# A message-passing kernel on one core: the turned table built first, and the shares of its column copies, row copies and gathers set anew

## The chip, the core and the metric

The kernel runs on one core of a Trainium2 chip. The metric is the device time of one execution in microseconds (us). A core has five engines with queues of their own: PE (matmul and transpose), DVE (VectorE), ACT (ScalarE), POOL (GpSimd) and SP, which here does nothing but issue DMAs. Each engine's sequencer takes its instructions in program order, loads registers and hands work to the engine.

## What is computed

```python
h = jnp.maximum(_layernorm(x, axis=-1), 0.0)          # 12500 nodes, 48 wide
x_i = h[dst]                                          # 400000 edges, dst sorted
x_j = h[src]
tmp = jnp.concatenate([x_i, x_j, edge_attr], axis=1)  # 48 + 48 + 32
msg = jax.nn.relu(tmp @ W1 + b1) @ W2 + b2            # hidden 128
out = x + jax.ops.segment_sum(msg, dst, num_segments=12500)
```

## The kernel before

**Tables first.** W1 splits in three. Ahead of the edges, `node_tables` normalizes the nodes in six slices (`centre`: mean and square; `scale`: variance, root, product), transposes them (`turn`, L170, into `ht`, with the ReLU) and multiplies: `table(j, wb, ...)` makes `tab_b`, the part by source, one row of 128 numbers for each node, `table(j, wa, ...)` makes `tab_a`, the part by destination with b1. Both go to DRAM through SP (L205). Beside that POOL gathers the raw x rows of the first chunks' edges (`xg`, L760), and turns `rel` into places inside a chunk's window. `squares`, `most` and `check` (L799 to L847) find out whether any edge lies outside its window and make addresses out of the index numbers.

**Edges in chunks.** Edges go in 391 chunks of 8 tiles of 128 (`T`, `CE`). Because dst is sorted, a chunk's destinations lie in a window of 80 nodes. For chunk c the loop of `windows` (L502) does, engine by engine in the order written there:

- SP (`prepare`, `rows`): loads of edge attributes (`lhs`), of destinations (`row`), of the window of `tab_a` (`rhs`), and one tile's share of row copies (`gs`, L289).
- POOL (L371): one indirect DMA for each tile that nobody else makes; it fetches 128 rows of `tab_b` into `gb`. `gp` has seven buffers.
- DVE: `lhs` (L379) one-hot of the window for the product with `rhs`, `hot` (L389) the same the other way round, `seg` (L460) the sum into the segment.
- PE: `before(c-1)` (L400) edge attributes and destination part into `pre`, `fold(c-2)` (L445, L448) the sum over edges into `p_g`, `gathered(c-1)` (L421) the source part added to `pre`.
- ACT: `hidden(c-1)` (L437), the ReLU.

**Four ways to the source part.** The source rows of a tile come in one of four ways. The first four chunks (`RAW`) take raw x, transposed and multiplied in the loop. All other tiles take a gather of POOL, row copies of SP (`gs`, 15 a chunk), or are built column by column out of `bt`, a copy of the table in SBUF with one column for each node: DVE and ACT each copy one column of 128 numbers for one edge (`columns`, L325 to L348). A chunk has 143 such copies in eleven parts (`PARTS`, L60): five on DVE (8, 15, 16, 20, 12) and six on ACT (12, 8, 8, 20, 12, 12). Ahead of each part the engine's own sequencer loads the part's addresses, one number for a copy, in multiples of four (L272); the place of the segment's sum is loaded with the part of 15. `bt` itself is made by `turn(i)` (L296), three blocks in each of the first chunks, out of `wb` and `ht`; copies start at chunk 5 (`COLS`).

**Segments.** Sums collect in two SBUF buffers (`segs`) by turns, twelve chunks each (`GQ`). At the change of segment DVE clears the new buffer (L476) and takes over the overlap (L478). During the next segment's first chunks PE multiplies the old one by W2 and b2 (L488, L489), DVE adds it to x (L495), SP stores it (L499).

The order of work on each engine is the order of the program (`manual_schedule`).

Of the kernel before, what the change touches and what calls it, by code (L numbers as in the profile page):

```python
# [40 lines left out]
RAW = 4  # L41
NRAW = RAW * T
RAW_PART = 16
# [8 lines left out]
TURNS = 3  # L52
BLOCKS = (NPAD + CE - 1) // CE
BUILD = (BLOCKS + TURNS - 1) // TURNS
COLS = BUILD
# [10 lines left out]
STRIP = 144  # L66
# [3 lines left out]
RPART = 15  # L70
BASE = 0

BT0 = 16512
SEG0 = 161696
# [3 lines left out]
AT_PLACE, AT_SEG, SEG, NEXT = 16, 17, 18, 19  # L78
WIDTH = 20
# [13 lines left out]
EPS = 1e-5  # L93

# [7 lines left out]
def node_tables(nc, tc, keep, x, ident, w1, b1, wb, ht, xg, ones, tab_a, tab_b, index, loads,  # L102
                squares, most, check):

    slices = [(0, 8), (8, 16), (24, 20), (44, 20), (64, 20), (84, 14)]
# [6 lines left out]
    with ExitStack() as es:  # L112
        node = es.enter_context(tc.tile_pool(name="node", bufs=3))
        sqp = es.enter_context(tc.tile_pool(name="sqp", bufs=2))
        ps_t = es.enter_context(tc.tile_pool(name="ps_t", bufs=3, space=PSUM))
        ps_n = es.enter_context(tc.tile_pool(name="ps_n", bufs=3, space=PSUM))
# [5 lines left out]
        wa = keep.tile([2 * D + 1, 2, HID], F32, name="wa")  # L122
        nc.vector.memset(wb, 0.0)
# [21 lines left out]
        sqs = {}  # L145

        def centre(j):
            r0, rb = slices[j]
            h = xs[j]
            of = total[:, r0 : r0 + rb]  # L150
            nc.vector.tensor_reduce(of, h, AX.X, ALU.add)
            nc.vector.scalar_tensor_tensor(
                h, of.unsqueeze(2).to_broadcast([P, rb, D]), -1.0 / D, h,
                op0=ALU.mult, op1=ALU.add,
            )
            sqs[j] = sqp.tile([P, rb, D], F32, name="sq")
            nc.scalar.activation(sqs[j], h, AF.Square)

        def scale(j):
            r0, rb = slices[j]  # L160
            h = xs[j]
            of = rstd[:, r0 : r0 + rb]
            var = node.tile([P, rb], F32, name="var")
            nc.vector.tensor_reduce(var, sqs.pop(j), AX.X, ALU.add)
            std = node.tile([P, rb], F32, name="std")
            nc.scalar.activation(std, var, AF.Sqrt, bias=eps, scale=1.0 / D)
            nc.vector.reciprocal(of, std)
            nc.vector.tensor_mul(h, h, of.unsqueeze(2).to_broadcast([P, rb, D]))

        def turn(j):  # L170
            r0, rb = slices[j]
            h = xs[j]
            for g in range(0, rb // 2, 4):
                n = min(4, rb // 2 - g)
                p_t = ps_t.tile([2 * D, 4, P], F32, name="p_t")
                for q in range(n):
                    nc.tensor.transpose(
                        p_t[:, q, :],
                        h[:, 2 * (g + q) : 2 * (g + q) + 2, :].rearrange("p r d -> p (r d)"),
                        ident,  # L180
                    )
                nc.scalar.activation(
                    ht[: 2 * D, r0 // 2 + g : r0 // 2 + g + n, :], p_t[:, :n, :], AF.Relu
                )

        def table(j, wt, tv, dve):

            r0, rb = slices[j]
            rows = wt.shape[0]
            t = node.tile([P, rb, HID], F32, name="tab")  # L190
            for g in range(0, rb // 2, 2):
                n = min(2, rb // 2 - g)
                p_n = ps_n.tile([P, 2, 2 * HID], F32, name="p_n")
                for q in range(n):
                    nc.tensor.matmul(  # L195
                        p_n[:, q, :], ht[:rows, r0 // 2 + g + q, :],
                        wt.rearrange("k a h -> k (a h)"), start=True, stop=True,
                    )
                to = t[:, 2 * g : 2 * (g + n), :].rearrange("p r h -> p (r h)")
                of = p_n[:, :n, :].rearrange("p q h -> p (q h)")  # L200
                if dve and g % 4:
                    nc.vector.tensor_copy(to, of)
                else:
                    nc.scalar.copy(to, of)
            nc.sync.dma_start(tv[:, r0 : r0 + rb, :], t)  # L205

        for i in range(ns + 3):
            if i < ns:
                centre(i)
            if 0 <= i - 1 < ns:  # L210
                scale(i - 1)
            if 0 <= i - 2 < ns:
                turn(i - 2)
            if i == ns:
                squares()
            if i == ns + 1:
                most()
            if i == ns + 2:
                check()
            if 0 <= i - 3 < ns:  # L220
                table(i - 3, wb, tb_v, i >= ns)
        late = {1: (centre, ns), 2: (scale, ns), 3: (centre, ns + 1), 4: (scale, ns + 1)}
        for j in range(ns):
            if j in late:
                of, k = late[j]
                of(k)
            table(j, wa, ta_v, True)


def windows(nc, tc, gp, bt, ident, idx, raw, rhss, x_t, tab_a, tab_b, dst, edge_t, w2s, b2s,  # L230
            sources, out_t):
# [3 lines left out]
    xg, wb, ht = raw  # L235
    with ExitStack() as es:
# [24 lines left out]
        gss = {}  # L261

# [30 lines left out]

        bt_v = bt.rearrange("h (p r) -> h r p", r=NR)

        def turn(i):  # L296

            n = min(T, NR - i * T)
            p_t = ps_p.tile([P, T, HID], F32, name="pre")
            parts = p_t.rearrange("h (k q) p -> h k q p", k=2)  # L300
            for k in range(2):
                nc.tensor.matmul(
                    parts[:, k, : n // 2, :].rearrange("h q p -> h (q p)"), wb[:, k, :],
                    ht[: 2 * D, i * T // 2 : (i * T + n) // 2, :].rearrange("k g p -> k (g p)"),
                    start=True, stop=True,
                )
            nc.scalar.copy(
                bt_v[:, i * T : i * T + n, :].rearrange("h (q k) p -> h q k p", k=2),
                parts[:, :, : n // 2, :].rearrange("h k q p -> h q k p"),
            )  # L310
# [14 lines left out]
        def columns(c, part):  # L325
# [15 lines left out]
            for k, of in enumerate(got[:n]):  # L341
                j, e = divmod(first + k, P)
                if j not in gts:
                    gts[j] = gtc.tile([HID, P], F32, name="gt")
                of = of.with_bounds(
                    min_val=BT0, max_val=BT0 + 4 * (N - 1), guaranteed_mod_val=0, out_of_modulus=4
                ) - BT0
                copy(gts[j][:, e : e + 1], bt8[:, bass.ds(of, 4)].bitcast(F32))  # L348

        def prepare(c):  # L350
# [10 lines left out]
            base, *nodes = numbers(c, BASE, 1 + m, mybir.EngineType.SP)  # L361
# [109 lines left out]
        def segment_next(g):  # L471

            old, new = segs[g % 2], segs[(g + 1) % 2]
            if g > 0:
                for k in range(2):
                    nc.vector.memset(new[:, k, W:], 0.0)  # L476
            of, = numbers(begin(g), NEXT, 1, mybir.EngineType.DVE)
            nc.vector.tensor_copy(  # L478
                new[:, :, :W], old[:, :, bass.ds(of.with_bounds(min_val=0, max_val=FAR), W)]
            )  # L480
# [20 lines left out]
        with tc.manual_schedule():  # L501
            for c in range(NCH + 2):  # L502
# [9 lines left out]
                columns(c, 1)  # L512
# [35 lines left out]
                for i in range(c * TURNS, min((c + 1) * TURNS, BLOCKS)):  # L548
                    turn(i)
# [130 lines left out]
def tile_gnn_preln(  # L680
# [15 lines left out]
    ones: bass.AP,  # L696
    w1: bass.AP,
# [38 lines left out]
    ht = const.tile([2 * D + 1, NR // 2, P], F32, name="ht")  # L736
# [11 lines left out]
    gp = ctx.enter_context(tc.tile_pool(name="gp", bufs=7))  # L748

    with tc.tile_pool(name="keep", bufs=1) as keep, tc.tile_pool(  # L750
# [14 lines left out]
        def loads():  # L765
# [12 lines left out]
            gather(0, RAW_PART)  # L778
# [7 lines left out]
            if NT > full * T:  # L786
# [3 lines left out]
                )  # L790

            nc.gpsimd.tensor_tensor(off[:, :2, :], far[:, 1:3, :], far[:, :2, :], op=ALU.subtract)
            nc.gpsimd.tensor_tensor(off[:, 2, :], off[:, 0, :], off[:, 1, :], op=ALU.add)
            nc.gpsimd.tensor_tensor(off[:, 3, :], off[:, 0, :], far[:, 3, :], op=ALU.add)
            nc.gpsimd.tensor_scalar_add(off, off, -MID)
            nc.gpsimd.tensor_tensor(far, off, off, op=ALU.mult)
            gather(RAW_PART, NRAW - RAW_PART)

        def squares():  # L799
# [135 lines left out]
```

## Time and profile before

| | us |
|---|---|
| median of 3 runs | 3365.4 (3362.72 to 3370.66) |
| the profiled execution | 3372.65 |
| its span, first to last instruction | 3370.8 |
| mean granted TensorE clock | 0.911 |

In the profile a group reads: line, engine, operation, tile written<-tiles read, shapes, xcount | busy us, mean ns of one | idle us of the engine just before them, and who ended it. A timeline row reads: start, duration, engine, line, operation, tiles, count and the idle time before it. A register load's row gives minimum, median and maximum in ns, then first and last start in us. "issue" is time in which nothing that the profile shows was waited for. Small instructions overlap at their ends: DVE's column copies show 144 ns each, but follow one another much faster.

### The profile page before, as it was taken

What the parts mean: (1) busy time and instruction counts of PE and PEld (TensorE: products, weight loads), DVE (VectorE), ACT (ScalarE), POOL (GpSimd) and SP (SyncE); (2) the same over time, 40 slices, a digit from 0 to 9 for tenths busy, and PEclk for the clock granted to TensorE, in tenths of its full rate; (3) what the DMA queues carried; (4) which work ended last, traced back from release to release, by engine and by line L of the source; (5) the groups of instructions that cost most, each with busy time, mean ns of one, the idle gap of its engine ahead of it and who ended that gap; (6) DMA issues with size and microseconds to landing.
All of it is one profiled execution on the core that took longest, in us unless ns stands there. A gap on an engine that the chain in (4) does not pass through costs nothing.

```text
span 3370.8 us, 115212 instructions
## 1 busy us (share of the span) xinstructions
PE 2775.6 (82%) x16394; PEld 2158.3 (64%) x16394; DVE 2800.1 (83%) x29140; ACT 3035.6 (90%) x28179; POOL 2530.0 (75%) x2670
## 2 busy tenths in 40 slices
PE   7987778888888888888887788888788788788777
PEld 6666666666666666666666666676666666666565
DVE  6588888888888888888888888888888888888876
ACT  5799998999998999998899999889998999999987
POOL 7677777777777777777777777777777777777776
PEclk9999998998898998988889999888998999899989
DMA  7433333333333333333333333333333333333333
GB/s 262 122 97 104 100 97 100 99 101 100 100 99 100 95 100 102 100 101 97 100 98 101 100 100 102 95 101 97 102 99 98 97 100 98 104 100 97 99 96 83
DMA packets 200234, 349.24 MB, mean 104 GB/s; under 512 B 69219, under 2 KB 107749, under 8 KB 198181
## 3 DMA queue, kind: packets, MB, share of 16 engines
q0 software_dynamic: 84800, 172.53, 18.9%
q1 hardware_dynamic: 114258, 169.09, 16.7%
q14 instruction: 634, 5.19, 0.5%
q8 instruction: 138, 2.26, 0.3%
q10 hardware_dynamic: 404, 0.17, 0.0%
HBM read 322.05 MB, written 22.07 MB: 102 GB/s over the span
## 4 chain that ended last, share of the span: by engine, by line
DVE 71%; issue 14%; PE 5%; DVEq 4%; POOL 2%; DMA 2%; ACT 0%; SPq 0%; POOLq 0%; ACTq 0%
DVE gt L348 47%; DVE lhs L379 12%; DVE hot L389 8%; DVEq L272 4%; DVE seg L460 2%; POOL gb L371 2%; PE pre L400 1%; PE p_g L445 1%; DVE xseg L495 1%; DVE seg L476 1%; DMA row<-in_dst 1%; PE p_f L488 1%; PE p_f L489 1%; DMA gb<-tab_b,srci 1%; PE p_n L195 1%
## 5 line engine op out<-in xcount | busy, mean ns | idle before, releaser
L371 POOL DMA_INDIRECT gb<-tab_b,srci x2618 | 2489.4, 951 | 812.7 <-issue 724.4
L348 ACT COPY gt<-bt 128x1 f32 x27705 | 2618.0, 188 | 63.9 <-issue 54.6
L348 DVE COPY gt<-bt 128x1 f32 x27335 | 1842.1, 144 | 463.3 <-issue 435.1
L400 PEld LDWEIGHTS pre<-rhs,lhs 112*128 112x128 f32 x6250 | 823.5, 208 | 277.1 <-issue 193.4
L400 PE MATMUL pre<-rhs,lhs 112*128 112x128 f32 x6250 | 841.5, 292 | 98.3 <-issue 56.7
L445 PE MATMUL p_g<-hot,hid 128*128 128x80 f32 x6250 | 794.0, 282 | 131.2 <-ACT hid L437 129.1
L445 PEld LDWEIGHTS p_g<-hot,hid 128*128 128x128 f32 x6250 | 758.4, 198 | 164.4 <-ACT hid L437 161.6
L421 PE MATMUL pre<-gb,ident 128*128 128x512 f32 (+2 forms) x1548 | 771.2, 627 | 34.3 <-DMA gb<-tab_b,srci 26.5
L437 ACT ACTIVATE hid<-pre 128x1024 f32<-128x1024 f32 x391 | 397.5, 1017 | 220.2 <-PE pre L421 205.8
L379 DVE TENSOR_SCALAR_CACHE_REDUCE lhs<-row,bw 80x1024 f32<-80x1024 int16 x391 | 494.6, 1265 | 14.8 <-DMA row<-in_dst 14.5
L421 PEld LDWEIGHTS pre<-gb,ident 128*128 128x128 f32 x1548 | 311.8, 225 | 281.0 <-issue 261.7
L421 PE MATMUL pre<-ident,gt 128*128 128x128 f32 x860 | 214.9, 336 | 261.7 <-DVE gt L348 234.7
L421 PEld LDWEIGHTS pre<-ident,gt 128*128 128x128 f32 x860 | 143.8, 210 | 291.5 <-issue 136.4
L389 DVE TENSOR_TENSOR hot<-wnum,rel 128x640 f32<-128x640 f32 x391 | 318.2, 814 | 0.0
L460 DVE TENSOR_TENSOR seg<-seg,p_g 128x160 f32 x391 | 121.5, 311 | 47.8 <-PE p_g L448 47.8
L448 PE MATMUL p_g<-ident,deg 80*128 80x80 f32 x782 | 156.4, 283 | 0.0
L448 PEld LDWEIGHTS p_g<-ident,deg 80*128 80x128 f32 x782 | 123.6, 198 | 0.0
L488 PE MATMUL p_f<-seg,w2s 128*48 128x512 f32 (+1 forms) x134 | 82.2, 700 | 44.3 <-DVE xseg L495 43.9
L489 PE MATMUL p_f<-seg,b2s 1*48 1x512 f32 (+1 forms) x134 | 76.2, 650 | 0.0
L488 PEld LDWEIGHTS p_f<-seg,w2s 128*48 128x48 f32 x134 | 12.3, 135 | 85.9 <-DVE xseg L495 60.0
L476 DVE MEMSET seg<- 128x944 f32 x64 | 54.1, 845 | 9.3
L489 PEld LDWEIGHTS p_f<-seg,b2s 1*48 1x48 f32 x134 | 11.3, 122 | 65.2 <-issue 65.2
(76 smaller groups left out, 429.0 us busy)
## 6 DMA issues: line engine op xcount, KB each, us to landing
gs<-tab_b SPq DMA_DIRECT2D x5760, 0.5 KB
row<-in_dst SPq DMA_DIRECT2D x390, 160.0 KB
lhs<-in_edge_t SPq DMA_DIRECT2D x390, 128.0 KB
gb<-tab_b,srci POOLq DMA_INDIRECT x2618
rhs<-tab_a SPq DMA_DIRECT2D x391, 40.0 KB
xseg<-in_x_t SPq DMA_DIRECT2D x33, 192.0 KB
out_x<-xseg SPq DMA_DIRECT2D x33, 192.0 KB
tab_b<-tab SPq DMA_DIRECT2D x3, 1280.0 KB
```

The source lines that it names most:

```text
L272: return nc.values_load_multi_w_load_instructions(table[c % P : c % P + 1, c // P, at : at + n], engines=[engine], min_val=0, max_val=1 << 23,
L348: copy(gts[j][:, e : e + 1], bt8[:, bass.ds(of, 4)].bitcast(F32))
L371: nc.gpsimd.indirect_dma_start(out=gb[:, t, :], out_offset=None, in_=tab_b[:, :], in_offset=bass.IndirectOffsetOnAxis(ap=srci[:, c * T + t ...
L379: nc.vector.tensor_scalar(lhs[:W, : n * P], row[:, : n * P], bw[:, c : c + 1], None, op0=ALU.is_equal, op1=ALU.add, accum_out=deg[:, :1],)
L389: nc.vector.tensor_tensor(hot[:, :n, :], wnum.unsqueeze(1).to_broadcast([P, n, W]), rel[:, c * T : c * T + n].unsqueeze(2).to_broadcast([P ...
L400: nc.tensor.matmul(pre[:, t, :], s["lhs"][:K, t * P : (t + 1) * P], s["rhs"][:K, :], start=t % BANK == 0, stop=False, skip_group_check=True,)
L421: nc.tensor.matmul(pre[:, t:e, :], lhsT, rhs, start=False, stop=True, skip_group_check=True)
L437: nc.scalar.activation(h[:, :n, :], s["pre"][:, :n, :], AF.Relu)
L445: nc.tensor.matmul(p_g[:, 0, :], s["h"][:, t, :], s["hot"][:, t, :], start=t == 0, stop=t == n - 1)
L448: nc.tensor.matmul(p_g[:, 1, :], s["deg"], ident[:W, :W], start=True, stop=True)
L460: nc.vector.tensor_add(to, to, s["p_g"])
L488: nc.tensor.matmul(p_f[:, :n], w2s, seg[:, 0, s], start=True, stop=False)
```

## The change

- **Turned table first.** `bt` moves into `node_tables`. `turned` makes it from `wb` and `ht` in groups of two, ACT copies it. Its columns are now in the order r x 128 + p instead of p x 98 + r. `back` transposes `bt` by PE into rows of `tab_b`; DVE and ACT take the copies by turns. `table(j, wb, ...)` and the loop's `turn(i)` go. `product` makes `tab_a` as before, two copies in five on DVE. Slices are 8 and five times 18. DVE's steps are cut up and strewn among PE's (`together`). `ht` lives only until the loop.
- **Checks.** The square of `rel` (ACT) and its maximum (DVE) become a maximum and a minimum of `rel` (DVE). The five small steps on `far` and `off` go from POOL to DVE. `addresses` works out the new column order for 4 x 152 numbers in each partition.
- **Five raw chunks.** `RAW` 5, 40 raw tiles (POOL gathers 16, then 24); copies start at chunk 4 and their tiles are used from chunk 5 on.
- **Shares.** DVE takes 72 copies in parts of 23, 16, 17, 16, ACT 76 in parts of 12, 16, 20, 12, 16; SP 16 row copies. `gp` has eight buffers.
- **SP's numbers.** Window bases for eight chunks are loaded at once, row numbers for two.
- **Sums cleared in pieces.** The memsets go; SP clears the old segment by eight DMAs from a row of zeros in DRAM, one in each of chunks 2 to 9 of a segment.

```diff
-RAW = 4
+RAW = 5
-RAW_PART = 16
+RAW_PART = 20
+RAW_EARLY = 16
-COLS = BUILD
+COLS = RAW - 1
 PARTS = (
-    (True, 0, 8), (True, 8, 15), (True, 24, 16), (True, 40, 20), (True, 60, 12),
-    (False, 72, 12), (False, 84, 8), (False, 92, 8), (False, 100, 20), (False, 120, 12),
-    (False, 132, 12),
+    (True, 0, 23), (True, 24, 16), (True, 40, 17), (True, 60, 16),
+    (False, 76, 12), (False, 88, 16), (False, 104, 20), (False, 124, 12), (False, 136, 16),
 )
-RPART = 15
-BASE = 0
+RPART = 16
+BASE, BASES = 2 * RPART, 8
+CLEAR = 8
-BYCOLS = tiles_of(COLS, PART)
+BYCOLS = [max(RAW, c) for c in tiles_of(COLS, PART)]
...
+        def turned(j, g):
+            r0, rb = slices[j]
+            n, at = min(2, rb // 2 - g), r0 // 2 + g
+            p_b = ps_n.tile([P, 4 * HID], F32, name="p_b")
+            parts = p_b[:, : 2 * n * P].rearrange("h (k q p) -> h k q p", k=2, q=n)
+            for k in range(2):
+                nc.tensor.matmul(
+                    parts[:, k, :, :].rearrange("h q p -> h (q p)"), wb[:, k, :],
+                    ht[: 2 * D, at : at + n, :].rearrange("k g p -> k (g p)"),
+                    start=True, stop=True,
+                )
+            nc.scalar.copy(
+                bt[:, 2 * at * P : 2 * (at + n) * P].rearrange("h (q k p) -> h q k p", k=2, q=n),
+                parts.rearrange("h k q p -> h q k p"),
+            )
+        def back(j, g):
+            r0, rb = slices[j]
+            n = min(4, rb - 2 * g)
...
+            for q in range(n):
+                at = (r0 + 2 * g + q) * P
+                nc.tensor.transpose(p_n[:, q * HID : (q + 1) * HID], bt[:, at : at + P], ident)
+            copy = nc.scalar.copy if g % 4 else nc.vector.tensor_copy
+            copy(tabs[j][:, 2 * g : 2 * g + n, :].rearrange("p r h -> p (r h)"), p_n[:, : n * HID])
...
+            if c % BASES == 0:
+                bases[:] = numbers(c, BASE, BASES, mybir.EngineType.SP)
+            if c % 2 == 0 and c + 1 >= ROWS0:
+                ahead[:] = numbers(c, 0, 2 * RPART, mybir.EngineType.SP)
...
-            if g > 0:
-                for k in range(2):
-                    nc.vector.memset(new[:, k, W:], 0.0)
+        def segment_clear(g, k):
+            n = 2 * (L - W) // CLEAR
+            half, at = divmod(k, CLEAR // 2)
+            nc.sync.dma_start(
+                segs[g % 2][:, half, W + at * n : W + (at + 1) * n],
+                zeros.unsqueeze(0).to_broadcast([P, n]),
+            )
...
                 columns(c, 0)
-                columns(c, 1)
                 segment_add()
                 if 0 <= c - 2 < NCH:
                     add(c - 2)
                     if k == GQ - 1:
                         segment_next(g)
-                columns(c, 2)
+                columns(c, 1)
                 if c < NCH:
                     compare(c)
                 if c < 2:
                     nc.vector.memset(segs[c], 0.0)
+                columns(c, 2)
                 columns(c, 3)
                 columns(c, 4)
                 columns(c, 5)
-                columns(c, 6)
-                columns(c, 7)
                 if 0 <= c - 1 < NCH:
                     gathered(c - 1)
                     hidden(c - 1)
+                columns(c, 6)
+                columns(c, 7)
                 columns(c, 8)
-                columns(c, 9)
-                columns(c, 10)
...
+                if g > 0 and begin(g + 1) < NCH and 0 <= k - STORE < CLEAR:
+                    segment_clear(g - 1, k - STORE)
...
-                for i in range(c * TURNS, min((c + 1) * TURNS, BLOCKS)):
-                    turn(i)
...
-    gp = ctx.enter_context(tc.tile_pool(name="gp", bufs=7))
+    gp = ctx.enter_context(tc.tile_pool(name="gp", bufs=8))
```

More of the change, by code (lines that the diff above doesn't have):

```diff
@@ L93 @@
 EPS = 1e-5
+ROUND = 1.5 * 2**23
 G = 5
@@ L99, with node_tables @@
 GNACC = 4
-def node_tables(nc, tc, keep, x, ident, w1, b1, wb, ht, xg, ones, tab_a, tab_b, index, loads,
-                squares, most, check):
-    slices = [(0, 8), (8, 16), (24, 20), (44, 20), (64, 20), (84, 14)]
+def node_tables(nc, tc, keep, x, ident, w1, b1, bt, wb, xg, ones, tab_a, tab_b, index, loads,
+                flags, check, addresses):
+    slices = [(0, 8)] + [(r0, 18) for r0 in range(8, NR, 18)]
     ns = len(slices)
@@ L162, in scale @@
             of = rstd[:, r0 : r0 + rb]
[L163 to L170, printed above, removed]
-            r0, rb = slices[j]
[L172 to L183, printed above, removed]
-                )
@@ L188, in table @@
+        def turned(j, g):
             r0, rb = slices[j]
[L189 to L204, printed above, removed]
@@ L210, in node_tables @@
             if 0 <= i - 1 < ns:
[L211 to L227, printed above, removed]
+                side += scale(i - 1)
@@ L261, in windows @@
         gss = {}
+        bases, ahead = [], []
         def group(c):
@@ L292, in rows @@
                 )
[L294 to L300, printed above, removed]
-            for k in range(2):
[L302 to L310, printed above, removed]
         def raw_turn(c):
```

253 lines of the change are left out of this document (178 added, 75 removed).

## The prediction

> **What bounds the kernel now.** First the page's totals and the chain of waits, then the stretch in which the chunk loop runs evenly (128 to 3134 us), grouped by engine, then one chunk on DVE and ACT.
>
> ```profile
> PE 2775.6 (82%) x16394; PEld 2158.3 (64%) x16394; DVE 2800.1 (83%) x29140; ACT 3035.6 (90%) x28179; POOL 2530.0 (75%) x2670
> ...
> DVE 71%; issue 14%; PE 5%; DVEq 4%; POOL 2%; DMA 2%; ACT 0%; SPq 0%; POOLq 0%; ACTq 0%
> ```
>
> ACT is the busiest, yet it has no share of the chain; DVE, its sequencer's loads (DVEq) and "issue" have 89%. The even stretch says why:
>
> ```profile
> L348 DVE COPY gt<-bt 128x1 f32 x25525 | 1720.1, 144 | 429.4 <-issue 404.5
> ...
> L348 ACT COPY gt<-bt 128x1 f32 x25877 | 2445.1, 188 | 58.3 <-issue 49.7 <-ACT gt L348 1.0
> L437 ACT ACTIVATE hid<-pre 128x1024 f32<-128x1024 f32 x360 | 366.2, 1017 | 181.1 <-PE pre L421 180.2 <-ACT gt L348 0.3
> ...
> L371 POOL DMA_INDIRECT gb<-tab_b,srci x2567 | 2441.2, 951 | 797.1 <-issue 708.8 <-DMA gb<-tab_b,srci 45.5 <-PE pre L421 29.4
> ...
> L379 DVE TENSOR_SCALAR_CACHE_REDUCE lhs<-row,bw x359: 1259/1266/1276, 132.1 to 3126.1; 80x1024 f32<-80x1024 int16 x180
> ```
>
> The last row gives the pace: one chunk in (3126.1 - 132.1)/358 = 8.363 us. DVE waits for nobody worth naming: its idle time stands before the column copies and is "issue". ACT has slack: it waits 180.2 us for PE, 180.2/359 = 0.50 us a chunk. A copy costs 1720.1/25525 = 67 ns on DVE and 2445.1/25877 = 94.5 ns on ACT. POOL's row (here from 128 to the end) has 0.31 us of idle time before each gather and hardly a wait besides; its stream reads:
>
> ```profile
> 52.62 0.95 POOL L371 DMA_INDIRECT gb<-tab_b,srci  x1 [0.34 <-issue]
> ...
> 127.82 0.95 POOL L371 DMA_INDIRECT gb<-tab_b,srci  x1 [12.98 <-PE pre L421]
> ...
> 3353.48 0.95 POOL L371 DMA_INDIRECT gb<-tab_b,srci  x1 [0.30 <-issue]
> ```
>
> One gather in 0.95 + 0.30 = 1.25 us, a stop of 12.98 us when all seven buffers are full, then without a break to 3353.48: (3353.48 - 127.82)/2566 = 1.257 us each. So two limits nearly coincide: DVE's pace by chunk, and POOL's stream, which ends 17.3 us before the span of 3370.8. To gain, the change must shorten both.
>
> What DVE's "issue" is, one chunk shows:
>
> ```profile
> 2011.89 0.82 DVE L348 COPY gt<-bt 128x1 f32 x12 [0.24 <-issue]
> 2012.63 1.27 DVE L379 TENSOR_SCALAR_CACHE_REDUCE lhs<-row,bw 80x1024 f32<-80x1024 int16 x1
> 2013.82 1.70 DVE L348 COPY gt<-bt 128x1 f32 x23
> 2015.44 0.32 DVE L460 TENSOR_TENSOR seg<-seg,p_g 128x160 f32 x1
> 2016.26 1.06 DVE L348 COPY gt<-bt 128x1 f32 x16 [0.51 <-issue]
> 2017.24 0.81 DVE L389 TENSOR_TENSOR hot<-wnum,rel 128x640 f32<-128x640 f32 x1
> 2018.21 1.30 DVE L348 COPY gt<-bt 128x1 f32 x20 [0.16 <-issue]
> 2020.10 0.82 DVE L348 COPY gt<-bt 128x1 f32 x12 [0.58 <-issue]
> ...
> 2009.37 6.75 ACT L348 COPY gt<-bt 128x1 f32 x72
> ...
> L272 DVEq TENSOR_LOAD <-cols x1: 598/598/598, 2012.4 to 2012.4; - x1
> L272 DVEq TENSOR_LOAD <-cols x1: 1102/1102/1102, 2015.1 to 2015.1; - x1
> L272 DVEq TENSOR_LOAD <-cols x1: 1351/1351/1351, 2016.8 to 2016.8; - x1
> L272 DVEq TENSOR_LOAD <-cols x1: 848/848/848, 2019.2 to 2019.2; - x1
> ...
> L272 ACTq TENSOR_LOAD <-cols x1: 546/546/546, 2013.6 to 2013.6; - x1
> L272 ACTq TENSOR_LOAD <-cols x1: 787/787/787, 2012.5 to 2012.5; - x1
> ```
>
> Before each part's copies the sequencer loads that part's addresses. The DVE rows are loads of 8, 16, 20 and 12 numbers, the ACT rows of 8 and 12. The time goes by the number: 63 ns each on DVE ((1351 - 598)/12), 60 ns on ACT ((787 - 546)/4), and hardly a fixed part (598 - 8 x 63 = 94 ns). A load is hidden only by what the engine still has queued: the 20 lies under hot's 0.81 and shows 0.16, the 16 behind seg shows 0.51, the 12 behind twenty copies shows 0.58 here (0.24 in the first row, the usual case). ACT shows no gap in 72 copies: its 12 are hidden by slower copies.
>
> **The change part by part: the chunk loop.** Tiles built by column go from 430 to (390 - 4) x 148 // 128 = 446, tiles by row (SP) from 45 to 48, raw tiles from 32 to 40; gathers of gb are 3125 - 446 - 48 - 40 = 2591 instead of 2618.
>
> *ACT* takes 76 copies a chunk instead of 72, in parts of 12 and 16 ahead of the relu, 20, 12 and 16 behind it. Four copies are 4 x 94.5 = 0.378 us. Two loads grow to 16 behind twelve copies: 546 + 8 x 60 = 1.02 us. What of it shows lies between nothing and 1.02 - 0.787 = 0.24, if the 12 are only just covered now. DVE's usual case sizes the cover: 0.848 less the 0.24 that shows is 0.61 us, nine copies; nine of ACT's are 0.85, so I take 0.16 twice, 0.32. Together 0.70 against 0.50 of slack: ACT becomes the longer engine, and the pace is 8.363 - 0.50 + 0.70 = 8.56 us. Bounds: no exposure, 8.24 (DVE then still decides); full, 8.72.
>
> The Trainium skill (Advanced Engine Details and Errata, Engine Queue Depths) gives ScalarE and VectorE a queue of 8: cover would be 8 x 94.5 = 0.756, each 16 would show 0.27, and the sum by it would be some 85 us more (2 x 0.11 x 386, an estimate). The hidden 787 ns loads speak against cover that small, so it stays out of the sum.
>
> *DVE* takes 72 copies instead of 71 (+0.07) in parts of 23, 16, 17 and 16, loads of 24, 16, 20 and 16. The 24 takes 94 + 24 x 63 = 1.60 and starts some 0.2 to 0.4 us ahead of lhs (1.19 to its successor): it shows 0 to 0.25, where the 8 and 15 it replaces show about 0.1. The 16 behind seg now follows 23 copies queued at once: 0.2 less to the same. The 20 is as before. The last 16 follows 17 copies instead of a 12 following 20: 1.102 - 0.848 = 0.25 more. The zeroing leaves DVE:
>
> ```profile
> 1329.95 0.31 DVE L460 TENSOR_TENSOR seg<-seg,p_g 128x160 f32 x1
> 1330.41 1.84 DVE L476 MEMSET seg<- 128x944 f32 x2
> 1332.16 0.18 DVE L478 COPY seg<-seg 128x160 f32 x1
> 1332.26 1.04 DVE L348 COPY gt<-bt 128x1 f32 x16
> ...
> 1331.48 1.66 POOL L371 DMA_INDIRECT gb<-tab_b,srci  x1 [0.30 <-issue]
> ```
>
> From seg's end to the copies are 2.00 us, but the memsets hide the segment's own load and the 16 (1.102), which then stand open: about 0.7 is won once in 12 chunks, 0.06 a chunk. Sum for DVE: +0.07 + 0 + (-0.1) + 0.25 - 0.06 = +0.16 (-0.05 to +0.4), 8.52. So DVE and ACT come out alike, and I take ACT's 8.56; for the pace 8.35 to 8.75 stays open.
>
> *SP* gets the sixteenth row copy and the clears; its rows:
>
> ```profile
> 2005.14 0.33 SPq L354 DMA_DIRECT2D lhs<-in_edge_t  x1
> ...
> 2007.68 4.91 SPq L289 DMA_DIRECT2D gs<-tab_b  x15
> ```
>
> From 2005.14 to 2012.59 SP works 7.5 us for a chunk; to it come one row copy (4.91/15 = 0.33) and eight clears in 12 chunks at about 0.45 with their setup (0.3), the loads staying about equal: 8.1, below 8.56. The row for the next chunk is issued first in each turn; cover is 0.4 us, and without it DVE's lhs would wait. Clears land in a buffer that nothing reads for several chunks. RAW's fifth chunk costs POOL eight gathers earlier, counted below.
>
> **The start.** The table by source now passes through two products in sequence.
>
> ```profile
> L195 PE MATMUL p_n<-wb,ht 96*128 96x256 f32 x98 | 25.3, 414 | 0.5 <-ACT tab L204 0.5
> ...
> 31.41 1.26 PE L177 MATMUL p_t<-ident,xs 128*96 128x128 f32 x10
> ...
> 88.83 1.98 PE L302 MATMUL pre<-ht,wb 96*128 96x512 f32 x4 [0.45 <-ACT bt L307]
> 90.74 2.05 PE L400 MATMUL pre<-rhs,lhs 112*128 112x128 f32 x16
> ...
> 96.37 0.60 PE L316 MATMUL p_f<-ident,xg 128*96 128x128 f32 x4
> ...
> 78.11 1.27 DVE L379 TENSOR_SCALAR_CACHE_REDUCE lhs<-row,bw 80x1024 f32<-80x1024 int16 x1 [7.68 <-DMA row<-in_dst]
> ...
> 119.84 1.27 DVE L379 TENSOR_SCALAR_CACHE_REDUCE lhs<-row,bw 80x1024 f32<-80x1024 int16 x1
> ```
>
> (The last row but one is the first chunk's lhs, the last is chunk 5's.) Ahead of the loop PE loses 25 us of wb products and gets the turned ones (100 passes of half a 512, 0.25 each: 25 us) and 98 transposes at 0.126: 12 us more, so the loop's first chunk comes at 78 + 12 = 90 (bounds +3, if ACT and DVE copies hide in PE's gaps, and +18, with DVE's second reduction over rel and address arithmetic open). In the loop the turns (L302) go, and PE needs from 90.74 to 96.97 = 6.2 us for a raw chunk without them: the first chunk with columns, now chunk 4, starts at 90 + 4 x 6.2 = 115 (before: chunk 5 at 119.84). The gathers of gb wait for the last tab_b store. They start unhindered at 52.62 now, so 12 us later the table is there by 64.6; POOL, with 8 raw gathers more, comes at 63: at most 2 us. The small steps on far and off go from POOL to DVE under PE's products, and bt's new column order changes addresses only.
>
> **The sum.** Columns run through 386 chunks, 4 to 389; 115 + 386 x 8.56 = 3419. From chunk 390 to the end it now takes 3370.8 - 3350.1 = 20.7:
>
> ```profile
> 3350.12 0.87 DVE L379 TENSOR_SCALAR_CACHE_REDUCE lhs<-row,bw 80x640 f32<-80x640 int16 x1
> ```
>
> 3440 against a span of 3370.8, +69. That profiled run took 3372.65, 7.25 over the median of 3365.4: forecast 3365.4 + 69 = 3434.
>
> **Rivals.** *The gathers decide (faster).* If both engines hide their larger loads, the end is POOL's: it has 8 raw gathers more and starts on gb at 52.6 + 10 = 63, needs 2591 x 1.25 = 3239 without the memsets (1.66 above for 0.95) and without the stop, and 17 to the end: 3319, 3313 by the median. It decides once the pace is below (3302 - 115)/386 = 8.26. For it: POOL really is full. Against: ACT must find 0.1 us where four copies alone ask 0.378 of its 0.50, and DVE has no slack. *The pace stays* (the larger loads hide, DVE wins the memsets and has its copy more, 8.37): 115 + 3231 + 21 = 3367, 3361 by the median, no change that can be told. *Both engines wait in turns*: all exposure open, 8.75: 115 + 3378 + 21 = 3514, 3508. SP would give nearly that, if the row copies and clears make lhs wait. *Fixed loads*: if a load cost the same whatever its size, nine in place of eleven would shed one of about 0.6 on each engine, and the gathers would decide: 3313. The four DVE rows rise in a straight line, so this holds little. The Trainium skill (DMA: Bandwidth & Descriptors, Latency and other measured facts) has such a rule, a floor of about 600 ns for a tensor load, amortized by unrolling; the 598 of eight numbers would agree, the 1351 of twenty doesn't.
>
> **How the numbers follow.** Forecast 0.60; gathers 0.12 and fixed loads 0.02 (both 3313); pace kept 0.11; waits in turns 0.15. About 0.2%, 7 us, is what a measurement can tell from no change. "Pace kept" falls to faster by 0.03, same by 0.05 and slower by 0.03; so faster 0.17, same 0.05, slower 0.78. The forecast's own range is 3385 to 3477 (pace 8.43 to 8.67); for eight in ten the range takes in "pace kept" and most of the waits: 3345 to 3500.
>
> **What would show it.** Right: lhs every 8.5 to 8.6 us from chunk 6 on; ACT's wait for PE below 0.2 us a chunk and its "issue" three times as long; a gap of about 0.5 before DVE's last 16; the stops of POOL for full buffers back in many places; first lhs near 90. Wrong: ACT's 76 copies without gaps, a pace at or below 8.37, or PE waiting for gb throughout (then the gathers decide); lhs waiting for row would be SP.

## The result: 6.8% slower, and SP's queue sets the pace

The changed kernel takes 3595.95 us (median of 4 runs, 3591.97 to 3597.67), the kernel before 3367.27 in the same comparison (3362.72 to 3370.66). The ratio is 1.0678, 95% interval 1.066 to 1.0697. The forecast of 3434 had the direction; the time lies above its range.

The page of the changed kernel: span, busy times, and the shares of the chain of waits by engine and by line.

```profile
span 3590.3 us, 117924 instructions
...
PE 2881.1 (80%) x16496; PEld 2251.2 (63%) x16496; DVE 2803.0 (78%) x29556; ACT 3228.9 (90%) x29780; POOL 2491.6 (69%) x2646
...
DVE 23%; SPq 22%; DMA 14%; PE 12%; issue 12%; ACT 10%; POOL 4%; DVEq 2%; ACTq 1%; POOLq 0%
DVE gt L393 14%; SPq L352 12%; DMA row<-in_dst 9%; ACT gt L393 9%; SPq L335 5%; DVE lhs L428 4%; PE pre L470 4%; POOL gb L420 4%; PE pre L449 4%; DMA rhs<-tab_a 2%; DVE hot L438 2%; SPq L399 2%; PE p_g L494 2%; DVEq L335 2%; ACT hid L486 1%
```

ACT has the same 90% as before and DVE less than its 83%. The chain has moved: SP's queue had 0% of it and now has 22%, chiefly by its row copies (L352, 12%) and its loads of numbers (L335, 5%); DMA had 2% and now has 14%, of which the landing of `row` is 9%. Busy shares don't show this, since SP's DMA issues aren't counted as busy.

Start and end in DVE's timeline (the first lhs, those of chunks 4 and 5, and the last):

```profile
91.42 1.27 DVE L428 TENSOR_SCALAR_CACHE_REDUCE lhs<-row,bw 80x1024 f32<-80x1024 int16 x1 [6.16 <-DMA row<-in_dst]
...
115.92 1.27 DVE L428 TENSOR_SCALAR_CACHE_REDUCE lhs<-row,bw 80x1024 f32<-80x1024 int16 x1 [5.11 <-DMA row<-in_dst]
125.40 1.27 DVE L428 TENSOR_SCALAR_CACHE_REDUCE lhs<-row,bw 80x1024 f32<-80x1024 int16 x1 [0.61 <-DMA row<-in_dst]
...
3569.50 0.86 DVE L428 TENSOR_SCALAR_CACHE_REDUCE lhs<-row,bw 80x640 f32<-80x640 int16 x1
```

First lhs at 91.4 (forecast 90), first chunk with columns at 115.9 (115), from the last chunk to the end 3590.3 - 3569.5 = 20.8 us (20.7). All the rest is pace: (3569.5 - 115.9)/386 = 8.95 us a chunk instead of the forecast 8.56, and 0.39 x 386 = 150 us is the whole miss in the span (3590.3 against 3440). The granted clock fell too, from 0.911 to 0.879, but a run below has the same 0.879 at 3437.3 us, so the clock is not what makes the rest.

The same even stretch as before (128 to 3134 us), by groups:

```profile
L393 ACT COPY gt<-bt 128x1 f32 x25495 | 2464.2, 187 | 114.4 <-issue 75.2 <-ACT gt L393 0.4 <-DVE gt L393 0.2
L420 POOL DMA_INDIRECT gb<-tab_b,srci x2252 | 2124.6, 943 | 881.9 <-issue 628.1 <-PE pre L470 226.9 <-DMA gb<-tab_b,srci 20.8
L393 DVE COPY gt<-bt 128x1 f32 x24163 | 1596.5, 144 | 543.8 <-issue 517.2 <-ACT gt L393 5.5
L428 DVE TENSOR_SCALAR_CACHE_REDUCE lhs<-row,bw 80x1024 f32<-80x1024 int16 x335 | 425.3, 1269 | 87.4 <-DMA row<-in_dst 81.1 <-DMA gs<-tab_b 4.8
L486 ACT ACTIVATE hid<-pre 128x1024 f32<-128x1024 f32 x336 | 341.2, 1015 | 126.9 <-PE pre L470 124.8 <-PE pre L460 1.2
```

DVE's lhs, which hardly waited (2.1 us for `row`), now waits 81.1 us for `row`: the sign that the prediction gave for SP ("lhs waiting for row would be SP"). POOL waits 226.9 us for PE where it was 29.4: its gathers no longer decide. ACT still waits for PE, 126.9/336 = 0.38 us a chunk, so ACT's longer list isn't the limit either.

SP's own timeline shows why `row` is late (start, duration, and x16 for sixteen row copies in a stretch):

```profile
1999.82 5.13 SPq L352 DMA_DIRECT2D gs<-tab_b  x16
2004.99 0.36 SPq L532 DMA_DIRECT2D seg<-in_zeros  x1
2005.47 0.36 SPq L399 DMA_DIRECT2D lhs<-in_edge_t  x1
2005.87 0.42 SPq L401 DMA_DIRECT2D row<-in_dst  x1
2006.70 0.33 SPq L413 DMA_DIRECT2D rhs<-tab_a  x1
2007.13 6.24 SPq L352 DMA_DIRECT2D gs<-tab_b  x16
2013.42 0.36 SPq L532 DMA_DIRECT2D seg<-in_zeros  x1
2013.89 0.42 SPq L399 DMA_DIRECT2D lhs<-in_edge_t  x1
2014.36 0.41 SPq L401 DMA_DIRECT2D row<-in_dst  x1
2017.67 0.33 SPq L413 DMA_DIRECT2D rhs<-tab_a  x1
2018.09 5.13 SPq L352 DMA_DIRECT2D gs<-tab_b  x16
```

There is hardly a pause in these rows: two chunks take 2018.09 - 1999.82 = 18.27 us. The hole from 2014.8 to 2017.6 is the loading of numbers. Chunks go in pairs now. One loads 32 row numbers (here the eight bases too) and then issues its copies in 5.13 us; the other loads nothing, and its sixteen copies take 6.24. The waits of SP's queue between 500 and 3200 us tell what the extra 1.1 us is. First the kernel before, then the changed one (waiter, whom it waited for, us in total, times, longest):

```profile
SPq L499 <- DVE seg L460: 115.1, 19, 10.3
SPq L499 <- DVE xseg L495: 50.7, 8, 9.2
SPq L289 <- DMA rhs<-tab_a: 8.3, 18, 0.9
```

```profile
SPq L352 <- DMA lhs<-in_edge_t: 47.6, 85, 1.5
SPq L352 <- DMA seg<-in_zeros: 43.3, 74, 1.5
SPq L352 <- DMA row<-in_dst: 26.5, 88, 0.6
SPq L554 <- DVE seg L509: 25.1, 20, 2.4
```

Before, SP came to the store of a segment (L499) too early and waited there, 165.8 us in all: that was its slack. Now 28.7 are left (25.1 and 3.6 for xseg). Instead its row copies (L352) wait for SP's own earlier transfers to land, 124.2 us with `rhs`. In the trace SP's DMAs use eight semaphores by turns, and a copy waits until the DMA eight places ahead of it has landed. A load of numbers between the big transfers (lhs, row, a clear) and the copies gives them time; in the chunk that loads nothing the copies come up behind them.

`row` is late behind the clears only: of the 87.4 us that lhs waits in the even stretch, 87.0 fall on the 224 chunks whose `row` SP issues behind a clear, 0.4 on the other 111. There the clear's issue comes first (some 0.4 us), and `row` lands later too: the last update of its semaphore comes 3.9 us after its issue, without a clear ahead 3.0 (medians, 500 to 3200 us).

### The profile page after: what moved, and what is told of

It reads as the page before. It is cut to its first block, busy times and chain, and to the rows that moved or that the text cites. A ratio compares the mean times of both kernels' runs of the same rounds, so it can differ in the third digit from the quotient of the medians.

```text
span 3590.3 us, 117924 instructions
## 1 busy us (share of the span) xinstructions
PE 2881.1 (80%) x16496; PEld 2251.2 (63%) x16496; DVE 2803.0 (78%) x29556; ACT 3228.9 (90%) x29780; POOL 2491.6 (69%) x2646
## 4 chain that ended last, share of the span: by engine, by line
DVE 23%; SPq 22%; DMA 14%; PE 12%; issue 12%; ACT 10%; POOL 4%; DVEq 2%; ACTq 1%; POOLq 0%
DVE gt L393 14%; SPq L352 12%; DMA row<-in_dst 9%; ACT gt L393 9%; SPq L335 5%; DVE lhs L428 4%; PE pre L470 4%; POOL gb L420 4%; PE pre L449 4%; DMA rhs<-tab_a 2%; DVE hot L438 2%; SPq L399 2%; PE p_g L494 2%; DVEq L335 2%; ACT hid L486 1%
## 5 line engine op out<-in xcount | busy, mean ns | idle before, releaser
L420 POOL DMA_INDIRECT gb<-tab_b,srci x2591 | 2445.0, 944 | 1011.9 <-issue 724.7
L393 ACT COPY gt<-bt 128x1 f32 x29296 | 2831.6, 187 | 129.4 <-issue 84.2
L449 PEld LDWEIGHTS pre<-rhs,lhs 112*128 112x128 f32 x6250 | 860.8, 216 | 327.3 <-issue 257.2
L449 PE MATMUL pre<-rhs,lhs 112*128 112x128 f32 x6250 | 879.1, 300 | 137.3 <-DVE lhs L428 112.3
L494 PE MATMUL p_g<-hot,hid 128*128 128x80 f32 x6250 | 810.1, 286 | 135.6 <-ACT hid L486 134.4
L494 PEld LDWEIGHTS p_g<-hot,hid 128*128 128x128 f32 x6250 | 778.0, 203 | 163.2 <-ACT hid L486 161.5
L470 PE MATMUL pre<-gb,ident 128*128 128x512 f32 (+3 forms) x1544 | 804.2, 655 | 0.0
L470 PE MATMUL pre<-ident,gt 128*128 128x128 f32 x892 | 234.5, 352 | 364.1 <-DVE gt L393 308.2
L470 PEld LDWEIGHTS pre<-gb,ident 128*128 128x128 f32 x1544 | 329.7, 236 | 254.9 <-issue 246.7
L550 DVE TENSOR_TENSOR xseg<-xseg,p_f 48x512 f32<-48x512 f32 (+1 forms) x67 | 44.7, 666 | 8.5 <-PE p_f L544 8.5
```

The lines of the kernel that those rows point to most:

```text
L420: nc.gpsimd.indirect_dma_start(out=gb[:, t, :], out_offset=None, in_=tab_b[:, :], in_offset=bass.IndirectOffsetOnAxis(ap=srci[:, c * T + t ...
L449: nc.tensor.matmul(pre[:, t, :], s["lhs"][:K, t * P : (t + 1) * P], s["rhs"][:K, :], start=t % BANK == 0, stop=False, skip_group_check=True,)
L470: nc.tensor.matmul(pre[:, t:e, :], lhsT, rhs, start=False, stop=True, skip_group_check=True)
L494: nc.tensor.matmul(p_g[:, 0, :], s["h"][:, t, :], s["hot"][:, t, :], start=t == 0, stop=t == n - 1)
```

## The experiments

Two figures describe each run. The **pace** is the mean distance of DVE's lhs from chunk 20 to 360. **SP's time** is what SP needs for a chunk: 2700 us (500 to 3200) less its waits for other engines, by the chunks in that stretch; the waits for its own transfers are in it and stand beside it. For the kernel before that is (2700 - 179.3)/322.4 = 7.82, for the changed one (2700 - 48.3)/301.5 = 8.79. SP's time and its waits for others make up the pace by definition; what tells is how little waiting is left, 0.16 us a chunk where it was 0.56. (Waits of less than 0.15 us are not listed and count as SP's time.)

| kernel | us | pace | SP's time | of it landing waits | loads of numbers |
|---|---|---|---|---|---|
| before | 3367.3 | 8.37 | 7.82 | 0.03 | 1.26 |
| changed | 3596.0 | 8.95 | 8.79 | 0.41 | 1.21 |
| changed, 8 row copies | 3466.0 | 8.61 | 5.75 | 0.45 | 0.75 |
| changed, memsets | 3444.6 | 8.54 | 8.20 | 0.12 | 1.20 |
| changed, 8 row copies, old shares | 3402.7 | 8.47 | 5.73 | 0.46 | 0.74 |
| before, SP's part | 3581.9 | 8.93 | 8.82 | 0.42 | 1.20 |
| before, new shares | 3437.3 | 8.56 | 7.81 | 0.05 | 1.26 |
| before, clears by SP | 3450.4 | 8.59 | 8.26 | 0.12 | 1.26 |
| before, clears by SP, 16 row copies | 3551.3 | 8.86 | 8.75 | 0.10 | 1.49 |
| changed, 15 row copies | 3588.1 | 8.92 | 8.72 | 0.40 | 1.45 |
| changed, clears in 2 pieces | 3521.6 | 8.76 | 8.47 | 0.32 | 1.21 |
| balanced | 3370.9 | 8.33 | 8.14 | 0.13 | 1.45 |

The kernel before took 3371.2, 3369.7 and 3371.8 beside these groups of runs. All but the first two rows and the last are single runs; kernels that ran several times spread by up to 0.4%, some 13 us, and smaller differences tell nothing. Eight further runs, of five of these kernels, fell where the kernel before took 5404.5 or 5323.6 us; no verdict rests on them.

**Is it SP's queue?** Half of its row copies taken away:

```diff
-RPART = 16
+RPART = 8
```

> The changed kernel with 8 row copies a chunk on SP instead of 16; POOL gathers 24 tiles more (2615). Theory S (SP's queue sets the pace: copies, clears and its waits for its own earlier DMAs fill 8.9 us a chunk): SP gets 8 x 0.36 = 2.9 us a chunk shorter, the pace falls from 8.95 to ACT's own 8.58 (8.24 of work, 0.33 of open loads), 386 x 0.37 = 143 us: 3595 to about 3450. Theory E (the larger parts of ACT and DVE cost it all, with PE passing their waits on): pace and time as they were, 3590 to 3600.

Measured 3466.0. Its SP waits:

```profile
SPq L554 <- DVE seg L509: 419.3, 22, 20.6
SPq L399 <- PE pre L449: 333.7, 134, 6.0
SPq L554 <- DVE xseg L550: 70.2, 4, 19.5
```

SP waits for other engines for a third of the stretch (896.9 of 2700 us), 130 us come back, and 8.61 is left, near the 8.56 that DVE and ACT had been given. lhs still waits 16.9 us in the even stretch, behind clears.

**Or the clears?** They go back to DVE, and SP keeps its 16 copies:

```diff
+            if g > 0:
+                for k in range(2):
+                    nc.vector.memset(new[:, k, W:], 0.0)
...
-                    segment_clear(g - 1, k - STORE)
```

> The changed kernel with the sums cleared by DVE's memsets as before instead of eight DMAs of SP. Theory S: SP loses 0.28 us a chunk of clears and some 0.15 of waits behind them, DVE gets 0.06 back: pace 8.55 to 8.65, 3440 to 3480. Theory E: 0.06 x 391 more, 3610 to 3625.

Measured 3444.6, 151 us less. The new shares of DVE and ACT alone make 3437.3 (below), and the changed kernel stands 159 us above that. Either edit alone brings most of the 159 back, so the two are no separate costs: each brings SP's time below the pace of the other engines.

**Which part does what.** The kernel before with SP's part alone (16 copies, numbers for two chunks at once, eight clears), and the kernel before with the new shares and order of DVE and ACT alone:

> The kernel before with nothing but SP's part of the change: 16 row copies, numbers loaded ahead, clears by DMAs. Theory S: pace 8.8 to 8.95 alone from this, 120 + 385 x 8.87 + 21: about 3545. Theory E: not slower than before, 3345 to 3370, as DVE loses the memsets.

> Once more the kernel before with the change's nine parts and their places, on a chip where the kernel before takes 3360 to 3380. The forecast's step for ACT and DVE by itself: pace 8.52 to 8.58, 3420 to 3445; 3480 and more if PE passes waits on; 3360 to 3375 if the larger loads are hidden.

SP's part alone costs 3581.9 - 3371.2 = 211 us, without a changed table or a new share, at a pace that theory S gave (8.93, in 8.8 to 8.95); its 3545 was added up wrongly, 120 + 385 x 8.87 + 21 is 3556. The new shares alone cost 3437.3 - 3369.7 = 68; the forecast had 69 for the whole change. Their sum, 279, is more than the change's 229: the longer of two queues decides, they don't add. The even stretch of the second:

```profile
L347 ACT COPY gt<-bt 128x1 f32 x26693 | 2578.9, 187 | 89.9 <-issue 50.7 <-DVE gt L347 0.4 <-ACT gt L347 0.2
...
L378 DVE TENSOR_SCALAR_CACHE_REDUCE lhs<-row,bw 80x1024 f32<-80x1024 int16 x351 | 444.4, 1266 | 0.4 <-DMA row<-in_dst 0.4
L436 ACT ACTIVATE hid<-pre 128x1024 f32<-128x1024 f32 x352 | 356.6, 1013 | 37.7 <-PE pre L420 37.3
```

lhs doesn't wait, and ACT's slack is down to 37.7/352 = 0.11 us a chunk from 0.50. The chain of waits, of which DVE had 71% and ACT 0%, is now shared:

```profile
DVE 45%; ACT 31%; issue 10%; PE 8%; DVEq 3%; ACTq 2%; DMA 1%; POOL 1%; SPq 0%
```

Both engines are full, as the forecast had them (8.52 and 8.56); which of them is the longer, this run doesn't tell.

**Both undone.** The changed kernel with 8 row copies and the old shares (143 copies in eleven parts, the old order):

> As the first run, and the column copies in the eleven parts and the places of before (143 a chunk; 2630 gathers). Both theories: no exposure of larger loads, DVE sets the pace at about 8.30 to 8.37, or the gathers the end (63 + 2630 x 1.25 + 17 = 3368): 3365 to 3385. What it tells is the difference to the first run: S says some 75 us for the parts (0.2 x 386), E says 210 or more.

3402.7, pace 8.47: above the range of both theories, and 63 less than the first run, near the 75 of theory S. Chunk by chunk, most of the 0.10 above the kernel before stands in the third chunk of a segment, where the store and the first clear are issued ahead of the next `row`: 10.27 us instead of 9.43. The two chunks ahead of it lose 0.5 together, the twelfth wins 0.44.

**The clears by themselves**, in the kernel before:

> Once more the kernel before with SP's eight clears in place of the memsets, on a chip where the kernel before takes 3360 to 3380. If SP's time counts: SP 7.88 + 0.28 + 0.2 = 8.36, pace 8.3 to 8.45, 3360 to 3410. If the clears hurt by their data: 3450 and more.

A miss for the sum over means: 3450.4 is what the second theory gave. SP's time, 8.26, is below the 8.37 of the other engines, yet the kernel is 81 us slower. The eight clears stand in eight of twelve chunks, ahead of each one's lhs and row, the first of them behind the store. DVE's waits in the even stretch of this kernel have a row that before stood at 2.1 us in 5 waits:

```profile
DVE lhs L380 <- DMA row<-in_dst: 45.1, 60, 1.9
```

The third chunk of a segment takes 10.09 us (9.43 before) and the tenth 9.12 (8.19); only the twelfth, free of the memsets, wins (8.88 for 9.38). SP still waits 105 us for other engines, but 74.9 of it at the store, once a segment: what it has gained on the others by then is lost there, and the clears come after.

The data of the clears has its part: here too `row` lands 3.9 us after its issue behind a clear and 3.0 without one, and all of lhs's waits (49.3 us) stand behind clears. But it hurts where SP comes late: with 8 row copies and the old shares (the run before this one) `row` lands as late, 4.0 for 3.1, yet lhs waits 19.9 us. How much of the 81 us is the clears' issue and how much their data was not taken apart.

**Number or bytes of the clears.** `CLEAR = 2` in the changed kernel makes two DMAs of 944 columns out of eight of 236 (the expectation names half of each width):

> The changed kernel with the clears in 2 pieces of 472 columns instead of 8 of 118 (the same bytes, six DMAs fewer in 12 chunks). If SP's time by the number of its DMAs is the cost: 6 x 0.42 / 12 = 0.2 us a chunk and the waits between them less, 3460 to 3520. If it is the data that the clears move: as the changed kernel, 3570 to 3600.

3521.6, just above the first range. Six DMAs fewer bring 74 us, so their number counts. But what stands behind the large pieces waits for longer. The row copies:

```profile
SPq L352 <- DMA seg<-in_zeros: 61.0, 25, 3.5
```

25 waits of 2.4 us instead of 74 of 0.6, though all landing waits together fall from 0.41 to 0.32 a chunk. And `row` lands 4.7 us after its issue behind such a piece (5.8 where the store is ahead as well): the bytes count too.

**One row copy less**, `RPART = 15`:

> The changed kernel with 15 row copies a chunk instead of 16. If SP's queue is over the pace (8.89 us of work a chunk), one copy of 0.33 and its wait come off the pace nearly in full: 8.55 to 8.65, 3465 to 3510. If SP is only late in places: 3570 to 3595.

3588.1, the rival's number and no more than the spread from 3596.0, but not for the rival's reason. The row copy's 0.33 did go; the loads grew by 1.45 - 1.21 = 0.24 a chunk. With 15 copies the bases begin at offset 30 of their row instead of 32. SP's loads in a chunk that has both, first here, then in the changed kernel (count, minimum/median/maximum in ns):

```profile
L335 SPq TENSOR_LOAD <-last x2: 1945/2061/2177, 2009.0 to 2011.0; - x2
```

```profile
L335 SPq TENSOR_LOAD <-last x2: 717/1292/1867, 2083.8 to 2084.5; - x2
```

Eight bases take 1945 ns instead of 717, and 30 numbers take longer (2177) than 32 (1867); the medians of 38 such pairs are 1883 for 728 and 2121 for 1922. Why a load that begins there is slow, no run shows.

**Numbers for one chunk at a time**, with 16 copies and the clears, in the kernel before:

> The kernel before with 16 row copies and SP's eight clears, the numbers loaded chunk by chunk as before. If the loading of 32 numbers for two chunks at once takes part in the loss (the chunk that has both loads is late): 8.7 to 8.85, 3495 to 3555, clearly below the 3582 of the kernel before with SP's whole part. If it does not: 3570 to 3595.

3551.3 against 3581.9 for SP's whole part. Loading two chunks ahead thus costs 31 us, though it saves 1.49 - 1.20 = 0.29 us of loads: 0.42 of landing waits stand in place of 0.10. That is the pair of rows 5.13 and 6.24 above. The sixteenth copy costs 0.33 plus 0.23, because 17 numbers take 1417 ns (median) where 16 take 1189.

**What is left when all is undone.** The turned table, five raw chunks and loading ahead stay; memsets, 15 row copies, and 143 column copies, 67 on DVE and 76 on ACT:

```diff
+    (True, 0, 8), (True, 8, 15), (True, 24, 16), (True, 40, 16), (True, 56, 12),
+    (False, 68, 12), (False, 80, 12), (False, 92, 8), (False, 100, 20), (False, 120, 12),
+    (False, 132, 12),
```

> The changed kernel with its turned table, five raw chunks and numbers loaded ahead, but with the clears by DVE's memsets, 15 row copies, and 143 column copies in the old order of the loop, of which DVE takes 67 and ACT 76. Theory (SP's queue and the larger loads each cost their own part; with SP below the pace and the loads small again nothing is left of the loss): a pace of 8.25 to 8.4, and POOL's stream of 2609 gathers decides with it: 63 + 2609 x 1.257 + 17 = 3360, so 3345 to 3385. Rival (the turned table or the numbers loaded ahead cost something in the loop themselves): 8.45 or more, 3400 and up.

3370.9 (10 runs) against 3371.8 (13 runs), ratio 0.9996, interval 0.9986 to 1.0005: no difference. Its pace of 8.33 is a little below the 8.37 of before, but POOL's stream decides the end:

```profile
65.73 0.94 POOL L421 DMA_INDIRECT gb<-tab_b,srci  x1 [5.13 <-DVE tab L250]
```

```profile
3344.68 0.94 POOL L421 DMA_INDIRECT gb<-tab_b,srci  x1 [0.30 <-issue]
```

2609 gathers from 65.73 to 3344.68 are 1.257 us each, as before, and the end comes 16.5 us later, at 3361.2 (worked out beforehand: 3360). ACT is close behind: the chain of waits has ACT at 35% and POOL at 17%. So the turned table, five raw chunks and loading ahead cost together nothing that shows, though a cost hidden under POOL's stream or made up by DVE's four copies less couldn't be told. No version tried beats the kernel before.

**The runs beside a slower kernel before.** A first set of four, where the kernel before took 5404.5 us: 15 row copies 5562.7, clears by SP 5428.5, clears and 16 row copies 5435.1, new shares 5505.5.

> The changed kernel with 15 row copies on SP instead of 16, nothing else. SP's work falls by 0.36 us a chunk, from 8.9 to about 8.55, next to ACT's 8.58. If SP's queue sets the pace up to that point: pace 8.6 to 8.7, 3465 to 3500. If the copies are free and the clears alone hold things up (by what waits behind their landing): 3570 to 3595.

> The kernel before with the eight clears of SP in place of the memsets, and nothing else. SP's 7.88 us a chunk becomes 7.88 + 0.28 + 0.2 of waits behind the clears = 8.36, DVE loses 0.06: pace 8.3 to 8.45, 3360 to 3410. If the clears hurt by their data rather than by SP's time (the DMA of 118 KB ahead of row and lhs), 3450 and more.

> As e6_before_clears with 16 row copies, SP's numbers still loaded chunk by chunk. SP 8.36 + 0.36 + 0.05 = 8.77: pace 8.75 to 8.9, 3520 to 3570. The difference to e4_before_sp (3582) is the loading ahead: nothing to 30 us in its favour by SP's time (0.05 a chunk), against it if the two loads in a row, 2.7 us ahead of rhs in each second chunk, stall what follows.

> The kernel before with the nine parts of the change (148 copies) and their places in the loop, nothing else: memsets, 15 row copies, four raw chunks. The step of the forecast for ACT and DVE by itself: pace 8.52 to 8.58, 120 + 385 x 8.55 + 21 = 3433, so 3420 to 3445. If the larger loads cost more than that, 3480 and more; if they are hidden, 3360 to 3375.

A second set, where it took 5323.6: 15 row copies 5491.2, clears by SP 5355.5, new shares 5429.4, clears in two pieces 5478.5.

> The kernel of e5_rows15 again, at a granted clock near 0.9 (there it was 0.72 and the kernel before took 5404 us): 15 row copies on SP instead of 16. If SP's queue sets the pace: SP 8.9 to about 8.55, next to ACT's 8.58, pace 8.6 to 8.7, 3465 to 3500. If the copies are free and the clears alone hold things up: 3570 to 3595.

> The kernel of e6_before_clears again at a clock near 0.9: the kernel before with SP's eight clears in place of the memsets. SP 7.88 + 0.28 + 0.2 = 8.36, DVE loses 0.06: pace 8.3 to 8.45, 3360 to 3410. If the clears hurt by their data rather than by SP's time, 3450 and more.

> The kernel of e8_before_newparts again at a clock near 0.9: the kernel before with the change's nine parts and their places. The forecast's step for ACT and DVE by itself: pace 8.52 to 8.58, 3420 to 3445; more than that if PE passes waits on (3480 and more), 3360 to 3375 if the larger loads are hidden.

> The changed kernel with its sums cleared by two DMAs of 472 KB a segment instead of eight of 118 KB: the same data, six issues less, and six times less a copy that waits for a clear's landing. If SP's time is what counts: three quarters of 0.28 + 0.15 come back, pace 8.58 to 8.65, 3460 to 3485. If the clears' data is what counts: 3570 to 3600.

All eight are inconclusive. The pace is over 13 us a chunk, and yet SP, with the same DMAs, waits for other engines in only 3 to 16% of the stretch (500 to 5000 us): it is slowed too. What is known of that stands in the last section.

## Why the prediction was wrong

**The step that failed** is SP's. It said: "From 2005.14 to 2012.59 SP works 7.5 us for a chunk; to it come one row copy (4.91/15 = 0.33) and eight clears in 12 chunks at about 0.45 with their setup (0.3), the loads staying about equal: 8.1, below 8.56." The measured time is 8.79, above 8.56. The terms:

- The 7.5 came from one chunk. The mean from 500 to 3200 us is 7.82: 0.3 missing. The segments' stores and loads, which that chunk didn't have, make 0.18 of it; the rest is spread over its rows.
- Row copy 0.33 and loads (1.21 for 1.26) were right; the clears measure 0.28 (201 of 373 ns and a 49 ns gap, by 301.5 chunks).
- Landing waits weren't in the sum: 0.41 against 0.03, 0.38 missing. 7.82 + 0.33 + 0.28 - 0.05 + 0.38 = 8.76.
- What the clears hold up was put at nothing: "Clears land in a buffer that nothing reads for several chunks." But `row` stands behind them in the queue and lands 3.9 us after its issue instead of 3.0, so lhs waits even where the sum stays below the pace (the kernel before with the clears: 8.26 of 8.37, and 81 us lost).

A sum that came out 0.46 under the bound, with "cover is 0.4 us" named in the next sentence, called for the mean of all chunks instead of one. The rival "Both engines wait in turns" held the mechanism ("SP would give nearly that, if the row copies and clears make lhs wait"), but its 8.75 was priced by DVE's and ACT's loads, so 3508 was too low and the range ended short of it.

What a late `row` does to DVE, its timeline shows:

```profile
2008.67 1.06 DVE L393 COPY gt<-bt 128x1 f32 x16 [0.61 <-issue]
2010.19 1.27 DVE L428 TENSOR_SCALAR_CACHE_REDUCE lhs<-row,bw 80x1024 f32<-80x1024 int16 x1 [0.46 <-DMA row<-in_dst]
2011.40 0.08 DVE L428 DVE_READ_ACCUMULATOR lhs<-row,bw 80x1 f32 x1
2011.94 1.49 DVE L393 COPY gt<-bt 128x1 f32 x23 [0.46 <-issue]
```

The wait is the sequencer's, so the load of the 24 addresses behind it starts late too. In the 103 chunks of the stretch in which lhs waits more than 0.3 us, DVE loses 0.80 there, and its gaps until the next lhs sum to 1.80 us; in the other 231 it is 1.58, with the new shares alone 1.42.

**What was right.** The start (90 and 115), the end (20.7), and the pace that DVE and ACT would have: 8.56, measured 8.556 with the new shares alone, which is partly luck (next paragraph). The gap of about 0.5 before DVE's last 16 is there (0.61 in the first row). The saving by the memsets, 0.7 once in 12 chunks, measures 0.5 (9.38 to 8.88). POOL's stops came back.

**Right in total, not in its parts:** ACT's 0.70. "Issue" before its copies hardly grew (50.7/351 for 49.7/359), so the loads of 16 open no such gaps; the forecast of three times as much was wrong. The group costs 2578.9/351.5 = 7.34 a chunk instead of 2445.1/359 = 6.81, 0.53 where four copies make 0.378: the copies overlap by about half, and a delay below some 90 ns (a copy shows 187 ns, the next follows after 94.5) shows as less overlap, not as a gap. With 0.09 of further idle time that is 0.62, and 0.11 of the slack was left.

## What to carry to other kernels

- A queue that only issues DMAs is an engine like the others: take its time as a mean over a whole period, from its slack at the point where it waits for others, before work is moved to it; here 8.56 - 7.82 = 0.74 us was left, and the new work took 0.56 and brought 0.38 of landing waits along.
- Mean slack isn't enough if the new work sits in some turns only: ask whether the queue can run ahead from the turns that have slack to those that have the load.
- Where transfers share a few completion semaphores, what stands between a large transfer and the small ones behind it (here a register load) may be cover; taking it away turns into waits.

## What the runs showed of the hardware

- A register load doesn't go by its count alone: on SP 16 numbers take 1189 ns and 17 take 1417, 32 take 2113, or 1922 right behind another load, and 8 take 728 or 1883 by where they begin (medians). The Trainium skill (Runtime: NRT & Kernel Launch, Instruction fetch mechanics) gives about 200 ns a register even in bulk, on a page that speaks of loads from HBM; these loads come from SBUF, and 2113/32 = 66 ns is a third of that.
- A DMA's row shows its issue alone. `row` is issued from 2005.87 to 2006.29, and DVE, waiting for it, starts at 2010.19, 3.9 us later. The Trainium skill (Perfetto Trace Analysis, DMA Instruction — HWDGE (DVE, Sync)) says so too: the data movement is not in the instruction's window.
- Where the kernel before took 5323.6 us (granted clock 0.73 instead of 0.88 to 0.91), the copies themselves were no slower, 187 and 145 ns, but DVE and ACT stopped at the same moments. The kernel before with the new shares there (span 5427.4 against 3435.4):

```profile
3003.03 0.21 DVE L347 COPY gt<-bt 128x1 f32 x2 [1.15 <-issue]
3003.04 0.28 ACT L347 COPY gt<-bt 128x1 f32 x2 [1.05 <-issue]
...
3003.75 0.19 ACT L347 COPY gt<-bt 128x1 f32 x1 [0.43 <-issue]
3003.75 0.15 DVE L347 COPY gt<-bt 128x1 f32 x1 [0.51 <-issue]
3004.46 0.22 DVE L347 COPY gt<-bt 128x1 f32 x2 [0.55 <-issue]
3004.47 0.19 ACT L347 COPY gt<-bt 128x1 f32 x1 [0.52 <-issue]
```

DVE and ACT resume within 10 ns of each other, again and again, after pauses that no wait explains. What holds both is open.
